# The last row tile of a decoder block behind its attention: halves on two engines, bf16 rows first

## The chip, the cores and the metric

The kernel runs on one core of a Trainium2 chip. A core has TensorE (PE, matrix products into PSUM), VectorE (DVE), ScalarE (ACT), GpSimd (POOL) and SyncE (SP, which here only starts transfers), each with its own stream of instructions; they wait for each other through semaphores. Sixteen DMA engines move data between the chip's memory and the on-chip SBUF. The metric is the device time of one execution in microseconds (us).

## The reference

Sixteen sequences of 112 rows (1792 rows in all, 1024 columns) go through three sub-layers. Each adds its result to its input and normalizes the row.

```python
x = _layernorm(x + _L0_attn_ref(x, w_gate, w_up, w_down))          # gated FF, half of each row set to 0
x = _layernorm(x + _L0_xattn_ref(x, ctx, ctx, Wq, Wk, Wv, Wo))     # 32 heads over 375 context rows
x = _layernorm(x + _L0_ffn_ref(x, qweight, qscale, qzeros))        # one 4-bit 1024x1024 matrix, in bf16

def _layernorm(x, axis=-1, eps=1e-05):
    m = jnp.mean(x, axis=axis, keepdims=True)
    v = jnp.var(x, axis=axis, keepdims=True)
    return (x - m) / jnp.sqrt(v + eps)
```

The last two of these lines end a row's work. The second one's output is rounded to bf16 for the third's matrix product, and is also added to that product in fp32.

## The kernel before, in words

The rows are cut into 14 tiles of 128 (`TT`), numbered 0 to 13. The program has one section after the other: gate, keys and values, up (`gates_keys_up`), down projection and first normalization (`Down`), and then `attention_and_ffn` (L772), which ends the kernel. A context manager, `as_written`, ties the instructions of each engine into the order in which the code writes them; so what stands ahead of an instruction on its engine is what the code wrote ahead of it.

`attention_and_ffn` goes over 128 units (sequence, half of the heads, one of four queries per key head). `scores` (L819), `normalize`, `square` and `values` (L876) are a unit's steps. When the sequences that fill a row tile are through, a `Tail` (L906) does the rest of that tile:

- `project` (L918) multiplies by `wo_sb`, a quarter of the columns at a time, and adds the result to the tile's fp32 row `xt`. For the last tile, number 13, `project_halves` (L933) does it in two parts, by the halves of the heads, into one PSUM tile `pp_last`; its two adds are at L944.
- `stats` (L946) calls `norm_stats` (L65): two `bn_stats` of 512 columns (L72), `bn_aggr` (L73) and the addition of `EPS` (L74) on VectorE, the power -0.5 on GpSimd (L75). GpSimd then makes `shift` = -mean * rstd (L949).
- `apply` (L953): ScalarE makes x * rstd + shift over all 1024 columns, in place in `xt` (L954).
- `normed` (L958): `apply`, then a VectorE cast of the row to bf16, `xb` (L961).
- `turn` (L963): TensorE transposes the eight 128-column parts of `xb` (columns j, j+8, ...) into one PSUM bank (L968); ScalarE copies the bank to `x2T` (L969).
- `packed` (L971): for each of two 512-column halves, eight bf16 matmuls `x2T` by `wf_sb` (L975), a ScalarE copy of the result to bf16 in `xb` (L980), and a GpSimd add to `xt` (L982).
- `stats` again, and `store` (L984): `apply`, and a 512 KB DMA of the tile to `out` from ScalarE's queue (L986).

For all tiles but the last, `piece` (L1011) and `lights` (L1031) hang these steps between the units: `behind` holds the matmul steps, `light` the others by the number of the unit behind which they are due.

Behind the last unit (L1081 and on) the order is written out by hand. The tiles 11 and 12 are finished there, and tile 13 begins. After `project_halves(1, pp)` come, in this order: tile 13's `stats` and `normed`; a loop that empties `behind` and `light`, which at this point holds tile 12's second `stats` and its `store`; tile 13's `turn`, `packed`, `stats` and `store`. PSUM banks come from a pool of three (`bank`, L800); `xb` and `x2T` have one buffer each.

Of the kernel before, what the change touches and what calls it, by code (L numbers as in the profile page):

```python
# [10 lines left out]
F32 = mybir.dt.float32  # L11
BF16 = mybir.dt.bfloat16
# [4 lines left out]
AF = mybir.ActivationFunctionType  # L17
ALU = mybir.AluOpType
# [4 lines left out]
P = 128  # L23
B, S, D = 16, 112, 1024
# [16 lines left out]
EPS = 1e-5  # L41
# [18 lines left out]
def layer_norm(nc, pool, y, out, negh):  # L60

    norm_apply(nc, y, out, *norm_stats(nc, pool, y, negh))


def norm_stats(nc, pool, y, negh):  # L65

    n = y.shape[0]
    st = pool.tile([P, 2, 6], F32, tag="ln_st", name="ln_st")
    mv = pool.tile([P, 2], F32, tag="ln_mv", name="ln_mv")
    rstd = pool.tile([P, 1], F32, tag="ln_rstd", name="ln_rstd")  # L70
    for i in range(2):
        nc.vector.bn_stats(st[:n, i, :], y[:, ts(i, D // 2)])  # L72
    nc.vector.bn_aggr(mv[:n], st[:n].rearrange("p a b -> p (a b)"))  # L73
    nc.vector.tensor_scalar(rstd[:n], mv[:n, 1:2], EPS, None, ALU.add)  # L74
    nc.gpsimd.tensor_tensor(rstd[:n], rstd[:n], negh[:n], ALU.pow)  # L75
    return mv[:n, 0:1], rstd[:n]


def norm_apply(nc, y, out, mean, rstd):
# [692 lines left out]
def attention_and_ffn(nc, tc, ident, ident_b, negh, x1_d, k_d, v_d, queries, wf_sb, wo, out):  # L772
# [16 lines left out]
    with ExitStack() as ctx:  # L789
# [4 lines left out]
        work = ctx.enter_context(tc.tile_pool(name="a_work", bufs=2))  # L794
        small = ctx.enter_context(tc.tile_pool(name="a_small", bufs=3))
# [4 lines left out]
        def bank():  # L800
            return ps.tile([P, 512], F32, tag="pg", name="bank")
# [104 lines left out]
        class Tail:  # L906
# [39 lines left out]
            def stats(self):  # L946
                mean, self.rstd = norm_stats(nc, small, self.xt, negh)
                self.shift = small.tile([P, 1], F32, tag="shift", name=f"shift_{self.t}")
                nc.gpsimd.tensor_scalar(  # L949
                    self.shift, mean, self.rstd, -1.0, ALU.mult, ALU.mult  # L950
                )
# [19 lines left out]
            def packed(self):  # L971
                for i in range(2):
# [8 lines left out]
                    x = self.xt[:, ts(i, 512)]  # L981
                    nc.gpsimd.tensor_tensor(x, x, yb, ALU.add)  # L982

            def store(self):  # L984
                self.apply()
                nc.scalar.dma_start(out[ts(self.t, P), :], self.xt)  # L986
                Tail.live -= 1
# [65 lines left out]
        for n in range(n_units):  # L1053
            b, c, r = units[n]
# [29 lines left out]
        n = n_units  # L1084
# [3 lines left out]
        tail = Tail(TT - 1)  # L1088
# [14 lines left out]
        values(n - 1)  # L1103
        step(n + 4)
        tail.project_halves(1, pp)
        tail.stats()
        tail.normed()
        n += 1
        n += 4
        while behind or light:  # L1110
            piece(n)
            lights(n)
            n += 1
        tail.turn()
        tail.packed()
        tail.stats()
        tail.store()


@with_exitstack  # L1120
def kernel(
# [34 lines left out]
    with as_written(nc, tc):  # L1156
        with ExitStack() as psum:
# [30 lines left out]
            for mc in range(EARLY):  # L1188
                queries.chunk(0, mc)
        attention_and_ffn(nc, tc, ident, ident_b, negh, x1_d, k_d, v_d, queries, wf_sb, wo, out)  # L1190


# [46 lines left out]
```

## Time and profile before

| | us |
|---|---|
| median of three runs | 2659.86 |
| the three runs | 2656.11, 2660.22, 2659.86 |
| the profiled execution, its own time | 2661.48 |
| its span, first to last instruction | 2659.7 |
| TensorE busy in the span | 2584.9 (97%) |
| VectorE, ScalarE, GpSimd busy | 1730.8, 1377.6, 1053.8 |
| end of tile 13's last projection matmul (L938), from the span's start | 2634.10 |
| start of tile 13's first matmul by `wf_sb` (L975) | 2644.82 |
| issue of the last store (L986) | 2655.95 |
| mean granted TensorE clock | 0.983 |

The page of a profile gives busy times, the chain of work that ended last (followed back from the end), and groups of instructions. A line of the view in order of time has the start in us from the start of the span, the duration in us, the engine (PEld is TensorE's weight load, a q behind the name its queue), the line of the code, the operation, what it writes and reads, the shapes, and in brackets how long the engine had been idle and which instruction ended that. A line of the groups has the engine, the operation, shapes and count, then the sum of busy time in us and the mean of one in ns, then the idle time before them. In the view by stretches of time the columns are named where it is shown.

### The profile page before, as it was taken

How to read it: one execution, taken by the hardware profiler on the slowest of the kernel's cores; microseconds unless marked ns; L12 is line 12 of the kernel's file. 1: busy time of each engine (PE TensorE's matmuls, PEld its weight loads, DVE VectorE, ACT ScalarE, POOL GpSimd, SP SyncE). 2: the span in 40 equal slices, each digit the busy share in tenths (PEclk: the TensorE clock that was granted, in tenths of full speed). 3: DMA queues.
4: the chain of work that ended last, by engine and by line, in shares of the span. 5: the costliest groups of instructions: out<-in, count | busy, mean ns of one | idle time of the engine just before them, and what ended most of it. 6: DMA issues, size and time to landing. Idle time of an engine off the chain costs nothing.

```text
span 2659.7 us, 33179 instructions
## 1 busy us (share of the span) xinstructions
PE 2584.9 (97%) x10266; PEld 1482.7 (56%) x10266; DVE 1730.8 (65%) x3579; ACT 1377.6 (52%) x2413; POOL 1053.8 (40%) x1097
## 2 busy tenths in 40 slices
PE   9999999999999999999999999998899999999997
PEld 4444444577776555555554444443556666667663
DVE  0478778866876788788730343158467777777773
ACT  0487787777767777787610000000255555565553
POOL 0002022213322444344450000023277888788783
PEclk9999999999999999999999999999889999999998
DMA  6221223154443543443346222166567777777763
GB/s 253 94 74 56 77 91 126 51 195 168 181 169 136 162 140 121 143 132 117 95 145 228 86 96 94 59 204 202 133 169 196 196 191 193 192 205 194 188 175 103
DMA packets 216960, 387.70 MB, mean 146 GB/s; under 512 B 32080, under 2 KB 151120, under 8 KB 212688
## 3 DMA queue, kind: packets, MB, share of 16 engines
q1 hardware_dynamic: 165456, 257.19, 32.3%
q0 software_dynamic: 35840, 100.59, 11.6%
q10 hardware_dynamic: 15488, 27.80, 3.5%
q8 instruction: 83, 1.36, 0.2%
q14 instruction: 93, 0.76, 0.1%
HBM read 208.36 MB, written 76.43 MB: 107 GB/s over the span
## 4 chain that ended last, share of the span: by engine, by line
PE 90%; DVE 3%; DMA 3%; ACT 2%; issue 1%; POOL 1%; ACTq 0%; SPq 0%; POOLq 0%; DVEq 0%
PE pg L146 20%; PE pu L234 19%; PE m L546 14%; PE bank L924 7%; PE pk L184 6%; PE pk L176 6%; PE bank L765 6%; PE sc L832 4%; PE po L887 3%; PE bank L975 2%; PE pt L255 1%; ACT probs L840 1%; DVE b L727 1%; DMA xr<-x_d 1%; DVE nmax L838 1%
## 5 line engine op out<-in xcount | busy, mean ns | idle before, releaser
L284 ACT ACTIVATE ja<-a,cand 128x1824 int8<-128x1824 f32 x434 | 788.6, 1817 | 178.4 <-DVE cand L296 174.4
L287 DVE TENSOR_SCALAR_CACHE_REDUCE jv<-a,cand 128x928 uint8<-128x928 f32 x434 | 510.0, 1175 | 56.9 <-ACT a L271 48.8
L234 PE MATMUL pu<-wu_sb,uxT 128*128 128x512 f32 (+1 forms) x1344 | 530.6, 548 | 0.0
L146 PE MATMUL pg<-wg_sb,gxT 128*128 128x456 f32 (+1 forms) x1344 | 519.9, 550 | 5.9 <-DMA wg_sb<-in_wg_dram 5.9
L840 ACT ACTIVATE probs<-sc,nmax 128x375 f32<-128x375 f32 x512 | 287.4, 573 | 237.6 <-DVE nmax L838 218.2
L146 PEld LDWEIGHTS pg<-wg_sb,gxT 128*128 128x128 f32 x1344 | 256.2, 191 | 268.8 <-issue 265.3
L849 POOL TENSOR_TENSOR probs<-probs,sums 128x1500 f32<-128x1500 f32 x128 | 344.2, 2689 | 142.4 <-DVE sums L848 123.2
L234 PEld LDWEIGHTS pu<-wu_sb,uxT 128*128 128x128 f32 x1344 | 249.0, 190 | 230.0 <-issue 188.4
L838 DVE TENSOR_REDUCE nmax<-sc 128x2 f32<-128x750 f32 x256 | 228.6, 932 | 150.3 <-PE sc L832 150.2
L546 PE MATMUL m<-wd,h 128*128 128x512 f32 (+1 forms) x616 | 268.0, 597 | 0.0
L860 DVE STREAM_TRANSPOSE squares<-probs 128x1536 f32<-128x1536 f32 x128 | 224.0, 1750 | 9.7 <-DMA weights<-squares 5.5
L155 POOL DMA_DIRECT2D s_d<-s x84 | 46.0, 548 | 427.4 <-DVE s L154 351.5
L765 PE MATMUL bank<-x1T,wq_sb 128*128 128x224 f32 x976 | 202.6, 361 | 0.0
L546 PEld LDWEIGHTS m<-wd,h 128*128 128x128 f32 (+1 forms) x616 | 117.5, 191 | 149.2 <-issue 145.1
L765 PEld LDWEIGHTS bank<-x1T,wq_sb 128*128 128x128 f32 x976 | 181.3, 191 | 33.2 <-issue 30.2
L924 PE MATMUL bank<-wo_sb,aT 128*128 128x256 f32 x832 | 195.0, 388 | 0.0
L758 ACT COPY x1T<-pq 128x448 f32<-128x448 f32 x4 | 2.0, 535 | 371.6 <-PE pq L757 371.6
L874 POOL DMA_DIRECT2D weights<-squares x320 | 178.6, 564 | 9.0 <-issue 6.6
L924 PEld LDWEIGHTS bank<-wo_sb,aT 128*128 128x128 f32 x832 | 155.4, 192 | 46.5 <-issue 24.9
L184 PE MATMUL pk<-wv_sb,ctx 128*128 128x256 f32 (+1 forms) x768 | 168.4, 379 | 0.0
L176 PE MATMUL pk<-ctx,wk_sb 128*128 128x375 f32 x512 | 164.4, 478 | 0.0
L184 PEld LDWEIGHTS pk<-wv_sb,ctx 128*128 128x128 f32 (+1 forms) x768 | 144.0, 188 | 24.8
(118 smaller groups left out, 2881.8 us busy)
## 6 DMA issues: line engine op xcount, KB each, us to landing
weights<-squares SPq DMA_DIRECT2D x704, 96.0 KB, 3.3
h<-hT_d SPq DMA_DIRECT2D x56, 640.0 KB, 4.5
weights<-squares POOLq DMA_DIRECT2D x320, 96.0 KB, 3.4
ctx<-in_ctxT_dram SPq DMA_DIRECT2D x16, 1500.0 KB, 6.7
a<-s_d SPq DMA_DIRECT2D x14, 1376.0 KB, 7.9
us<-s_d SPq DMA_DIRECT2D x56, 256.0 KB, 2.7
hT_d<-hT POOLq DMA_DIRECT2D x56, 256.0 KB, 3.1
s_d<-s POOLq DMA_DIRECT2D x56, 228.0 KB, 2.2
```

The costliest lines, as they stand in the source:

```text
L146: nc.tensor.matmul(pg[:, :w], xts[t][:, kc, :], wg_sb[:, kc, ds(off, w)], start=(kc == 0), stop=(kc == KC - 1),)
L176: nc.tensor.matmul(pk[:, :SK], wk_sb[:, kc, ts(u, P)], c[:, kc, :], start=(kc == 0), stop=(kc == KC - 1),)
L184: nc.tensor.matmul(pk[:n, :KVD], c[:, kc, ds(at, n)], wv_sb[:, kc, :], start=(kc == 0), stop=(kc == KC - 1),)
L234: nc.tensor.matmul(pu[:, :w], xts[t][:, kc, :], wu_sb[0][:, kc, ds(off, w)], start=(kc == 0), stop=(kc == KC - 1),)
L284: nc.scalar.activation(ja, a[:, NV:], AF.Sign, bias=cand, scale=-1.0, accum_out=st["sgn"])
L287: nc.vector.tensor_scalar(jv, a[:, :NV], cand, -(TOPK - 1 - NA / 2), ALU.is_lt, ALU.add, accum_out=st["nlt"])
L546: self.nc.tensor.matmul(bank, a[:r, k, :], b(k)[:r], start=(k == 0), stop=(k == HK - 1),)
L765: nc.tensor.matmul(pq[:, :GT], self.wq_sb[:, kc, ts(mc, P)], self.x1T[g][:, kc, :], start=(kc == 0), stop=(kc == KC - 1),)
L838: nc.vector.tensor_reduce(nmax[h], sc[h][:, :, :SK], AX.X, ALU.max, negate=True)
L840: nc.scalar.activation(pr[:, i, :SK], sc[i // 2][:, i % 2, :SK], AF.Exp, bias=nmax[i // 2][:, i % 2 : i % 2 + 1], accum_out=sums[:, i : i ...
L849: nc.gpsimd.tensor_tensor(pr, pr, sums.unsqueeze(2).to_broadcast([P, 4, SK]), ALU.mult)
L924: nc.tensor.matmul(pp[:, :256], aT[:, h, r, :], wo_sb[:, h * REP + r, ts(i, 256)], start=(h == 0 and r == 0), stop=(h == 1 and r == REP - 1),)
```

## The change

`norm_stats` is cut in two: the part behind the `bn_stats` is now `norm_of`. After `project_halves(1, pp)` the loop over `behind` and `light` comes first, without the two steps of the count ahead of it, and then one new method, `last`, does all that is left of tile 13:

- `stats`, unchanged.
- The bf16 row `xb` comes straight from the fp32 row: ScalarE makes the first 512 columns, VectorE the other 512, both as x * rstd + shift. `xt` keeps its unnormalized values for now.
- The eight transposes go to two PSUM banks, four to each. ScalarE copies the first to `x2T[:, :4]`, VectorE the second to `x2T[:, 4:]`.
- The fp32 row is normalized in place behind that, again by halves on ScalarE and VectorE.
- For each 512-column half: eight matmuls, ScalarE's copy to bf16, an add on VectorE (not GpSimd), and that half's `bn_stats` right behind it.
- The last normalization by halves on ScalarE and VectorE, and two stores of 256 KB: the first half from ScalarE's queue, the second from SP's.

Other tiles are done as before. In the line numbers of the changed kernel, `last` is L988 to L1040.

```diff
+            def last(self):
+                n = D // 2
+                self.stats()
+                self.xb = work.tile([P, D], BF16, tag="xb", name="xb_last", bufs=1)
+                nc.scalar.activation(
+                    self.xb[:, :n], self.xt[:, :n], AF.Identity, bias=self.shift, scale=self.rstd
+                )
+                nc.vector.tensor_scalar(
+                    self.xb[:, n:], self.xt[:, n:], self.rstd, self.shift, ALU.mult, ALU.add
+                )
+                self.x2T = work.tile([P, 8, P], BF16, tag="x2T", name="x2T_last", bufs=1)
+                by_place = self.xb.rearrange("t (p j) -> t j p", j=8)
+                for h in range(2):
+                    pt = bank().bitcast(BF16)[:, : 4 * P].rearrange("p (j t) -> p j t", j=4)
+                    for j in range(4):
+                        nc.tensor.transpose(pt[:, j, :], by_place[:, 4 * h + j, :], ident_b)
+                    if h:
+                        nc.vector.tensor_copy(self.x2T[:, 4:], pt)
+                    else:
+                        nc.scalar.copy(self.x2T[:, :4], pt)
+                nc.scalar.activation(
+                    self.xt[:, :n], self.xt[:, :n], AF.Identity, bias=self.shift, scale=self.rstd
+                )
+                nc.vector.tensor_scalar(
+                    self.xt[:, n:], self.xt[:, n:], self.rstd, self.shift, ALU.mult, ALU.add
+                )
+                st = small.tile([P, 2, 6], F32, tag="ln_st", name="ln_st_last")
+                for i in range(2):
+                    pf = bank()
+                    for j in range(8):
+                        nc.tensor.matmul(
+                            pf, self.x2T[:, j, :], wf_sb[:, j, ts(i, n)],
+                            start=(j == 0), stop=(j == 7),
+                        )
+                    yb, x = self.xb[:, ts(i, n)], self.xt[:, ts(i, n)]
+                    nc.scalar.copy(yb, pf)
+                    nc.vector.tensor_add(x, x, yb)
+                    nc.vector.bn_stats(st[:, i, :], x)
+                mean, self.rstd = norm_of(nc, small, st, negh)
...
+                nc.scalar.activation(
+                    self.xt[:, :n], self.xt[:, :n], AF.Identity, bias=self.shift, scale=self.rstd
+                )
+                nc.scalar.dma_start(out[ts(self.t, P), :n], self.xt[:, :n])
+                nc.vector.tensor_scalar(
+                    self.xt[:, n:], self.xt[:, n:], self.rstd, self.shift, ALU.mult, ALU.add
+                )
+                nc.sync.dma_start(out[ts(self.t, P), n:], self.xt[:, n:])
...
         tail.project_halves(1, pp)
-        tail.stats()
-        tail.normed()
-        n += 1
-        n += 4
         while behind or light:
             piece(n)
             lights(n)
             n += 1
-        tail.turn()
-        tail.packed()
-        tail.stats()
-        tail.store()
+        tail.last()
```

More of the change, by code (lines that the diff above doesn't have):

```diff
@@ L65, in norm_stats, with norm_of @@
 def norm_stats(nc, pool, y, negh):
-    n = y.shape[0]
     st = pool.tile([P, 2, 6], F32, tag="ln_st", name="ln_st")
+    for i in range(2):
+        nc.vector.bn_stats(st[:, i, :], y[:, ts(i, D // 2)])
+    return norm_of(nc, pool, st, negh)
+def norm_of(nc, pool, st, negh):
     mv = pool.tile([P, 2], F32, tag="ln_mv", name="ln_mv")
     rstd = pool.tile([P, 1], F32, tag="ln_rstd", name="ln_rstd")
[L71 to L76, printed above, removed]
+    nc.vector.bn_aggr(mv, st.rearrange("p a b -> p (a b)"))
+    nc.vector.tensor_scalar(rstd, mv[:, 1:2], EPS, None, ALU.add)
+    nc.gpsimd.tensor_tensor(rstd, rstd, negh, ALU.pow)
+    return mv[:, 0:1], rstd
 def norm_apply(nc, y, out, mean, rstd):
@@ L982, in packed @@
                     nc.gpsimd.tensor_tensor(x, x, yb, ALU.add)
+            def last(self):
[25 more added lines that the diff above has]
+                st = small.tile([P, 2, 6], F32, tag="ln_st", name="ln_st_last")
+                for i in range(2):
+                    pf = bank()
[9 more added lines that the diff above has]
+                mean, self.rstd = norm_of(nc, small, st, negh)
+                self.shift = small.tile([P, 1], F32, tag="shift", name="shift_last")
+                nc.gpsimd.tensor_scalar(
+                    self.shift, mean, self.rstd, -1.0, ALU.mult, ALU.mult
+                )
[5 more added lines that the diff above has]
+                    self.xt[:, n:], self.xt[:, n:], self.rstd, self.shift, ALU.mult, ALU.add
+                )
+                nc.sync.dma_start(out[ts(self.t, P), n:], self.xt[:, n:])
```

## The prediction

> **What bounds the kernel now.** I read the page first, then the chain that ended last from 2560 us on, then the instructions in order of time from 2628 us to the end, then the groups with shapes kept apart, then the granted clock by stretches. The page says that the kernel as a whole belongs to TensorE:
>
> ```profile
> PE 90%; DVE 3%; DMA 3%; ACT 2%; issue 1%; POOL 1%; ACTq 0%; SPq 0%; POOLq 0%; DVEq 0%
> ```
>
> The reader is to see that little but PE ends the chain. The change touches nothing until the last projection matmul ends at 2634.10 us. All that it can win or lose lies in the 25.6 us from there to the end of the span, 2659.70 us, where one row tile is left and the engines work one behind the other:
>
> ```profile
> 2634.13 0.69 DVE L944 TENSOR_TENSOR x<-x,pp_last 128x512 f32<-128x512 f32 x1 [3.79 <-PE pp_last L938]
> 2634.73 1.28 DVE L72 BATCH_NORM_STATS2 ln_st<-x 128x6 f32<-128x512 f32 x2
> ...
> 2637.47 1.24 ACT L954 ACTIVATE x<-x,shift,ln_rstd 128x1024 f32<-128x1024 f32 x1 [10.67 <-POOL shift L949]
> 2638.74 0.69 DVE L961 CAST xb<-x 128x1024 bf16<-128x1024 f32 x1 [2.30 <-ACT x L954]
> 2639.35 1.28 DVE L72 BATCH_NORM_STATS2 ln_st<-x 128x6 f32<-128x512 f32 x2
> ...
> 2642.09 1.24 ACT L954 ACTIVATE x<-x,shift,ln_rstd 128x1024 f32<-128x1024 f32 x1 [3.39 <-POOL shift L949]
> 2643.37 0.34 ACTq L986 DMA_DIRECT2D out_dram<-x  x1
> 2643.75 1.01 ACT L969 COPY x2T<-bank 128x1024 bf16<-128x1024 bf16 x1 [0.42 <-ACT x L954]
> 2644.82 0.13 PEld L975 LDWEIGHTS <-x2T 128*128 128x128 bf16 x2 [4.50 <-ACT x2T L969]
> 2644.82 5.82 PE L975 MATMUL bank<-wf_sb,x2T 128*128 128x512 bf16 x16 [4.26 <-ACT x2T L969]
> ...
> 2651.34 1.15 POOL L982 TENSOR_TENSOR x<-x,xb 128x512 f32<-128x512 f32 x1 [1.06 <-ACT xb L980]
> 2652.52 0.69 DVE L72 BATCH_NORM_STATS2 ln_st<-x 128x6 f32<-128x512 f32 x1 [1.51 <-POOL x L982]
> ...
> 2654.67 1.24 ACT L954 ACTIVATE x<-x,shift,ln_rstd 128x1024 f32<-128x1024 f32 x1 [3.41 <-POOL shift L949]
> 2655.95 0.34 ACTq L986 DMA_DIRECT2D out_dram<-x  x1
> ```
>
> Three things are to be seen. The eight transposes end at 2639.49 + 1.07 = 2640.56 us, but their copy starts at 2643.75 us: ScalarE takes its work in order, and ahead of that copy stands the store of tile 12 (2642.09), which waits for statistics that VectorE began at 2639.35. That is 3.2 us of the path. Second, whole rows are done by one engine where two could share them (1.24, 0.69, 1.01, 1.24). Third, 9.05 us lie between the last matmul's end (2644.82 + 5.83 = 2650.65) and the end.
>
> **The change, step by step.** Times below are span times of the changed kernel, with the stretches of before where the shape stays.
>
> Up to the shift. Tile 12's statistics now stand ahead of tile 13's on VectorE, behind the same adds at L944. Tile 12 so takes the slots 2634.73 (bn_stats) to 2637.47 (ScalarE apply) that tile 13 had, and tile 13's bn_stats starts when L74 is issued: 2636.29 + 0.08 (at 2591.36 the next instruction followed L74 by 0.08) = 2636.37, which is **1.64 later**. Its shift releases ScalarE at 2637.47 + 1.64 = 2639.11. ScalarE meanwhile applies tile 12 (1.24) and issues its store, 2638.75 to 2639.09: it is free as the shift arrives, at 2639.13. Nobody waits for tile 12's store.
>
> The bf16 halves. The forms that give the prices:
>
> ```profile
> L954 ACT ACTIVATE x<-x,shift,ln_rstd 128x1024 f32<-128x1024 f32 x28 | 35.0, 1250 | 20.2 <-POOL shift L949 20.2
> L980 ACT CAST xb<-bank 128x512 bf16<-128x512 f32 x28 | 16.4, 591 | 14.5 <-PE bank L975 14.3
> L969 ACT COPY x2T<-bank 128x1024 bf16<-128x1024 bf16 x14 | 14.3, 1019 | 15.7 <-PE bank L968 15.2 <-ACT x L954 0.4
> L80 DVE TENSOR_SCALAR y<-y,ln_mv,ln_rstd 128x1024 f32<-128x1024 f32 x14 | 11.4, 813 | 9.9 <-POOL ln_rstd L75 9.9
> ```
>
> ScalarE at 512 against 1024 columns: 1.019 - 0.591 = 0.43 less, so the half apply is 1.25 - 0.43 = **0.82** (bounds 0.62, the half, and 1.25). VectorE's half: the 1024-column cast takes 0.69 and a 128-column one (L719) 0.22, 0.52 ns a column, so 0.81 - 0.27 = 0.54 (bounds 0.41 and 0.81). It lies beside ScalarE's half, which ends last: 2639.13 + 0.82 = 2639.95. In the built program neither half waits for the other.
>
> Transposes from 2640.00, as before 0.05 behind their input. Four end after 3 x 0.107 + 0.32 = 0.64 (0.107 is the spacing of the eight in 1.07). ScalarE's copy of half a bank is 0.59 (L980): 2640.68 to 2641.27, and the first matmul starts at **2641.33** instead of 2644.82. VectorE's copy of the other half, bounded by 0.35 (half a cast) and 0.69 (L944, which reads PSUM too), is wanted by the fifth matmul, 1.7 us later: hidden. The fp32 halves (0.82 and 0.54) lie beside the matmuls; without that cover they would cost 0.82. Gain so far 2644.82 - 2641.33 = **3.49**.
>
> The matmuls depend on the granted clock:
>
> ```profile
> 1935.90:1939.31 3.41, 3.41 (x11) 2.98 (x10) 2.77 (x4) 2.34 (x8) 1.99 (x1) 0.50 0.58 129
> ...
> 2639.06:2642.46 3.40, 1.07 (x8) 0.82 (x8) 1.93 (x5) 0.36 (x1) 0.81 (x2) 0.50 0.00 0
> 2642.46:2645.87 3.41, 1.05 (x3) 0.43 (x4) 0.00 (x0) 1.89 (x2) 0.00 (x0) 0.50 0.38 156
> 2645.87:2649.28 3.41, 3.41 (x9) 1.21 (x8) 0.00 (x0) 0.59 (x1) 0.16 (x1) 0.50 0.00 0
> ```
>
> Columns: stretch, length, busy time of PE, its loads, VectorE, ScalarE, GpSimd, granted clock, DMA. The clock is 0.50 until a stretch of 3.41 is all busy, and 1.00 in the next (from 2649.29; at 1929.07 and 1932.49 stretches with 3.09 and 2.87 busy were not enough, the one at 1935.90 was). A matmul is 0.427 apart at 0.50 and 0.227 at full clock (16 in 3.63). On the same grid of stretches the changed kernel's first full one is 2642.46 to 2645.87: 4.54 / 0.427 = 10.6 matmuls slow, 5.4 x 0.227 = 1.2 after it, 5.8 in all, as before. End 2647.16; gain here 0. Bounds, if the grid falls otherwise: 4.6 (a stretch that starts with the transposes) and 6.9 (16 x 0.427).
>
> Behind the matmuls. The first half's copy, add and bn_stats (0.59 + 0.68 + 0.69) hide beside the second half's matmuls. For the second: copy 0.59, then the add on VectorE, 0.68 (512-column fp32 tensor_tensor, L241 and L562; bounds 0.68 and GpSimd's 1.15), bn_stats 1.35 behind the last matmul where it was 2652.52 - 2650.65 = 1.87: gain **0.52**. From bn_stats to the apply 2.15, unchanged. The half apply on ScalarE 0.82 for 1.24; VectorE's ends at 0.54 and so issues the SP half first: 1.35 + 2.15 + 0.54 + 0.05 = 4.09 behind the last matmul, ScalarE's half at 4.36, where the whole store went at 5.30. SP has been idle since 2616. The store's packets ran from 2656.75 to about 2658.2 at 399 GB/s and below, 0.85 behind the issue; the span ended 3.75 behind it. I let the two halves share this rate, so the end is 4.09 + 3.75 = 7.84 behind the last matmul against 9.05: gain 1.21 (with the 0.52). If each had the full rate, it would be 0.4 less. [...]
>
> **Sum:** 3.49 + 0 + 1.21 = **4.7 us**. The profiled execution took 2661.48 (span 2659.70 and 1.8 around it), so it would take 2656.8. It lies 1.6 above the median of the three runs, 2659.86, which are 4.1 apart; on the median the forecast is 2659.86 - 4.7 = **2655.2**. What a measurement here can tell from no change is 0.2%, 5.3 us: the bounds are 2654.5 and 2665.2, and the forecast lies 0.7 inside.
>
> **Rivals.**
> 1. *The clock comes earlier.* If the grid falls so that one stretch holds the transposes and the matmuls (only 0.26 idle between them, where before had 4.26), the matmuls take down to 4.6: gain 4.7 + 1.2 = 5.9, time 2654.0. For: a grid that does not start with the kernel. Against: a stretch 3.09 of 3.42 busy was not enough. [...] No stretch here decides it.
> 2. *Halves cost what wholes do.* Apply halves of 1.25 (twice 0.43) and a late clock (6.9 - 5.8 = 1.1): gain 4.7 - 2.0 = 2.7, time 2657.2. Against: 0.59 and 1.02 for the two widths.
> 3. *The end is a late store.* The last half lands late on SP's queue. Price: the rows' longest landing of a 512 KB store is 9.0 us (L672) against 2.6 for the last one here, 6.4: time 2655.2 + 6.4 = 2661.6, slower; it decides from a landing of 2.6 + 4.7 = 7.3 us. For: two queues on one set of engines. Against: the DMA column is 0 ahead of it.
>
> That the change does less than it says is no rival: the built order has tile 12's store ahead and the halves apart.
>
> **How the numbers follow.** Forecast as summed (gain 4.0 to 5.3) 0.50, rival 1 0.30, rival 2 0.15, rival 3 0.05. Faster by over 0.2%: rival 1 and, since medians of runs 4 us apart scatter by about 1, a third of the forecast: 0.47. Within: the rest of the forecast, rival 2, part of rival 3: 0.50. Slower: 0.03. Range: low 2655.2 - 1.2 (clock) - 0.4 (halves of 0.62) - 0.4 (store) - 1.2 (scatter) = 2652.0; high 2657.2 + 0.8 (scatter) = 2658.0. Rival 3 is left out.
>
> **What would show it.** Tile 12's ScalarE apply near 2637.5, then the half at L994 near 2639.1 of 0.82; first L1020 matmul 7.2 behind the last L938 one; L1026 of 0.68; SP's issue 0.3 ahead of ScalarE's. I am wrong if the halves of L994 take over 1 us, if the 16 matmuls are far from 5.8, or if work ahead of 2634 moves.

## The result and the profile after

| | before | after |
|---|---|---|
| median of 22 runs each, us | 2657.57 | 2654.11 |
| lowest to highest | 2654.92 to 2663.45 | 2648.84 to 2657.43 |
| the profiled execution, its own time | 2661.48 | 2652.74 |
| its span | 2659.67 | 2650.93 |
| start of tile 13's last projection add (L944, L948) | 2634.13 | 2629.37 |
| from there to the end of the span | 25.55 | 21.55 |

The changed kernel is 3.46 us faster by the medians; the ratio on record is 0.9986, with a 95% interval from 0.998 to 0.9993. The interval lies below 1, so the change is faster; but the gain is smaller than the 0.2% that the prediction set as the least that can be told from no change here. The two profiled executions differ by more, 8.74 us, but 4.76 of it lies ahead of the last projection add, in instructions that the change doesn't touch. In the 13 kernels profiled for this study that add starts anywhere from 2628.35 to 2635.27 us. So the start is set aside as scatter, and everything below is measured from that add: the tail went from 25.55 to 21.55, **4.0 us less**.

The page's shares of the chain that ended last say the same as before, PE 89% for 90%, and can't show a change of 4 us. The view in order of time of the changed kernel, from the add to the end, answers to the first lines shown of before (columns as there):

```profile
2629.37 0.69 DVE L948 TENSOR_TENSOR x<-x,pp_last 128x512 f32<-128x512 f32 x1 [3.79 <-PE pp_last L942]
...
2632.72 1.24 ACT L958 ACTIVATE x<-x,shift,ln_rstd 128x1024 f32<-128x1024 f32 x1 [10.67 <-POOL shift L953]
...
2633.99 0.34 ACTq L1044 DMA_DIRECT2D out_dram<-x  x1
...
2634.35 0.55 DVE L997 TENSOR_SCALAR xb_last<-x,ln_rstd,shift 128x512 bf16<-128x512 f32 x1 [1.03 <-POOL shift L953]
2634.44 0.81 ACT L994 ACTIVATE xb_last<-x,shift,ln_rstd 128x512 bf16<-128x512 f32 x1 [0.48 <-POOL shift L953]
...
2635.31 1.07 PE L1005 MATMUL bank<-ident_b,xb_last 128*128 128x128 bf16 x8 [5.97 <-ACT xb_last L994]
2635.99 0.59 ACT L1009 COPY x2T_last<-bank 128x512 bf16<-128x512 bf16 x1 [0.74 <-PE bank L1005]
...
2636.63 4.45 PE L1020 MATMUL bank<-wf_sb,x2T_last 128*128 128x512 bf16 x10 [0.25 <-ACT x2T_last L1009]
...
2642.57 0.59 ACT L1025 CAST xb_last<-bank 128x512 bf16<-128x512 f32 x1 [1.73 <-PE bank L1020]
2643.20 0.69 DVE L1026 TENSOR_TENSOR x<-x,xb_last 128x512 f32<-128x512 f32 x1 [0.89 <-ACT xb_last L1025]
...
2646.08 0.82 ACT L1033 ACTIVATE x<-x,shift_last,ln_rstd 128x512 f32<-128x512 f32 x1 [2.92 <-POOL shift_last L1030]
2646.08 0.55 DVE L1037 TENSOR_SCALAR x<-x,ln_rstd,shift_last 128x512 f32<-128x512 f32 x1 [1.03 <-POOL shift_last L1030]
2646.66 0.35 SPq L1040 DMA_DIRECT2D out_dram<-x  x1
2646.93 0.34 ACTq L1036 DMA_DIRECT2D out_dram<-x  x1
```

Three things are to be seen. The copy of the transposes (L1009) no longer waits for tile 12: it starts 0.68 behind the first transpose, where before it stood 3.2 behind the last. The matmuls start 7.26 behind the add, where before it was 10.69. And between SP's issue and the end of the span there are 4.27 us, where before 3.73 lay behind the issue of the whole store.

The tail falls into three stretches: from the add to the first matmul by `wf_sb`, from there to the copy of the second half's result, and from there to the end. This table holds them for all kernels. Its last two columns are about the closing, the instructions behind the kernel's own work; the trace has them, most of them DRAIN and EVENT_SEMAPHORE, under one line at the program's end, L1286 in the changed kernel. `SyncE` is the time from the end of GpSimd's last computing instruction, the second `shift` of tile 13, to the end of SyncE's last closing instruction, which stands behind the landing of the stores (2649.63 in the changed kernel, where the later store landed 2.4 behind its issue at 2646.93). `closing` is the time from there to GpSimd's next instruction.

| kernel | to the first matmul | matmuls | copy to end | whole tail | SyncE | closing |
|---|---|---|---|---|---|---|
| before | 10.69 | 5.85 | 9.00 | 25.55 | 4.27 | 0.03 |
| after | 7.26 | 5.94 | 8.35 | 21.55 | 3.59 | 0.56 |
| e1_order | 9.28 | 5.03 | 9.00 | 23.31 | 4.27 | 0.03 |
| e2_halves | 9.04 | 5.15 | 8.35 | 22.54 | 3.59 | 0.57 |
| e3_early12 | 5.54 | 6.08 | 8.36 | 19.98 | 3.58 | 0.57 |
| e4_warm | 7.08 | 3.66 | 8.35 | 19.09 | 3.59 | 0.56 |
| e5_act_store | 7.26 | 5.29 | 8.35 | 20.90 | 3.86 | 0.29 |
| e6_one_store | 7.25 | 6.20 | 8.35 | 21.80 | 3.85 | 0.31 |
| e7_sp_store | 7.25 | 5.98 | 8.35 | 21.57 | 3.84 | 0.31 |
| e8_pool_add | 7.25 | 5.91 | 8.85 | 22.01 | 3.59 | 0.56 |
| e9_all | 4.89 | 3.66 | 8.35 | 16.90 | 3.60 | 0.55 |
| e10_act_end | 7.25 | 5.86 | 8.49 | 21.59 | 4.26 | 0.03 |
| e11_two_stores | 10.69 | 6.14 | 9.07 | 25.90 | 4.35 | 0.03 |

Where the work is the same, the first and the last stretch repeat to within 0.02 (7.25 and 7.26 in six kernels, 8.35 and 8.36 in eight; that three of these eight store in another way is taken up below). So single profiles can be compared there. A few matmul records are missing from the traces, so a line can count 15 of 16. The matmuls scatter with the clock, from 5.03 to 6.20 where nothing holds it up, and are read apart.

### The profile page after: what moved, and what is told of

The parts are those of the page before. It is cut to its first block, busy times and chain, and to the rows that moved or that the text cites. A ratio compares the mean times of both kernels' runs of the same rounds, so it can differ in the third digit from the quotient of the medians.

```text
span 2650.9 us, 33174 instructions
## 1 busy us (share of the span) xinstructions
PE 2579.0 (97%) x10252; PEld 1480.9 (56%) x10266; DVE 1732.0 (65%) x3584; ACT 1376.4 (52%) x2414; POOL 1051.7 (40%) x1095
## 4 chain that ended last, share of the span: by engine, by line
PE 89%; DVE 3%; DMA 3%; ACT 2%; issue 1%; ACTq 1%; POOL 0%; SPq 0%; POOLq 0%; DVEq 0%
PE pu L238 19%; PE pg L150 19%; PE m L550 14%; PE bank L928 7%; PE pk L188 6%; PE pk L180 6%; PE bank L769 6%; PE sc L836 4%; PE po L891 3%; PE bank L979 2%; PE pt L259 1%; ACT probs L844 1%; DMA xr<-x_d 1%; DVE nmax L842 1%; DMA wq_sb<-in_wq_dram 1%
```

## The experiments

The theory was that the first stretch gains from two things, the order (nobody waits for tile 12) and the halves, that the clock gives nothing, and that the end gains less than forecast. The rivals were that one of the two does it all, and that the second queue or VectorE's late half costs the rest.

**The order alone, and the halves alone.** In e1_order the kernel before gets only the new order:

```diff
-        tail.stats()
-        tail.normed()
-        n += 1
-        n += 4
         while behind or light:
...
+        tail.stats()
+        tail.normed()
         tail.turn()
```

In e2_halves the changed kernel has the old order: `last` is cut behind the bf16 halves, and its first part stands ahead of the loop.

```diff
         tail.project_halves(1, pp)
+        tail.first()
         while behind or light:
...
         tail.last()
```

> The kernel before with the order alone changed: tile 12's second statistics and its store stand ahead of tile 13's statistics; tile 13 is still done by whole rows. I measure in the profile the stretch from the start of the last projection add (L944) to the first matmul by wf_sb (10.69 us before, 7.26 in the changed kernel) and from that add to the end of the span (25.5 and 21.6). Theory: order and halves are two gains that add. The order takes 3.2 of ScalarE's wait away and costs 1.64 of VectorE's time, so the first matmul comes at 10.69 - 1.5 = 9.2 and the end at about 24.0. Rival: the order is the whole of the gain ahead of the matmuls and the halves are hidden: 7.3 and about 22.3. Second rival: the order alone gains nothing, as tile 13 starts 1.64 later and whole rows eat the rest: 10.7 and 25.5.

> The changed kernel with the old order: tile 13's statistics and its bf16 halves first, then tile 12's statistics and store, then the transposes' copies and all the rest by halves. Theory (two gains that add): tile 13's halves are ready 1.64 earlier than in the changed kernel, but ScalarE's copy of the first transposes stands behind tile 12's apply and store again; add to first matmul 8.9 us (a gain of 1.8 on 10.69), end at 23.2. Rival (order is the whole gain): 10.7 and 24.8. Rival (halves are the whole gain): 7.3 and 21.6.

To the first matmul e1 took 9.28 and e2 9.04: gains of 1.41 and 1.65, together 3.06, where both at once gain 3.43. Their own times were 2655.75 and 2656.52, with 2658.95 for a run of before beside them. The view in order of time of e1, around the transposes:

```profile
2634.00 1.24 ACT L954 ACTIVATE x<-x,shift,ln_rstd 128x1024 f32<-128x1024 f32 x1 [10.67 <-POOL shift L949]
...
2635.74 1.24 ACT L954 ACTIVATE x<-x,shift,ln_rstd 128x1024 f32<-128x1024 f32 x1 [0.50 <-POOL shift L949]
2637.01 0.69 DVE L961 CAST xb<-x 128x1024 bf16<-128x1024 f32 x1 [2.41 <-ACT x L954]
...
2637.76 1.07 PE L968 MATMUL bank<-ident_b,xb 128*128 128x128 bf16 x8 [7.14 <-DVE xb L961]
2638.87 1.01 ACT L969 COPY x2T<-bank 128x1024 bf16<-128x1024 bf16 x1 [1.89 <-PE bank L968]
```

Tile 12's apply (2634.00) is out of the way, and the copy follows the transposes; but whole rows stand one behind the other, 1.24, 0.69 and 1.01. The same view of e2:

```profile
2635.52 0.81 ACT L994 ACTIVATE xb_last<-x,shift,ln_rstd 128x512 bf16<-128x512 f32 x1 [10.68 <-POOL shift L953]
...
2636.39 0.71 PE L1010 MATMUL bank<-ident_b,xb_last 128*128 128x128 bf16 x8 [4.25 <-ACT xb_last L994]
...
2638.91 1.24 ACT L958 ACTIVATE x<-x,shift,ln_rstd 128x1024 f32<-128x1024 f32 x1 [2.58 <-POOL shift L953]
...
2640.57 0.59 ACT L1014 COPY x2T_last<-bank 128x512 bf16<-128x512 bf16 x1 [0.42 <-ACT x L958]
```

Here the transposes end at 2637.10, and the copy waits until 2640.57 for tile 12's apply and store. Two gains are left. VectorE's half no longer waits for ScalarE's whole row, so that tile 12's shift comes 6.71 behind the add (2638.88 - 2632.17) where before it was 7.94, 1.23 earlier; and the copy takes 0.59 for 1.01. That is 1.65. So both parts gain, and neither rival (the order alone, the halves alone) holds.

**What is still on the path.** In e3_early12 the loop that ends tile 12 stands ahead of `project_halves(1, pp)`, so that its statistics lie beside the last projection matmuls:

```diff
-        tail.project_halves(1, pp)
         while behind or light:
             piece(n)
             lights(n)
             n += 1
+        tail.project_halves(1, pp)
         tail.last()
```

> The changed kernel with the loop for tile 12 moved ahead of the last projection, so that tile 12's statistics and store lie beside TensorE's projection matmuls instead of ahead of tile 13's statistics. Theory: the changed kernel's order pays 1.64 us of VectorE's time on the path; here it is hidden, but the first of the two adds may start up to 0.15 late: add to first matmul 7.26 - 1.64 = 5.6, end at about 20.0 (clock as in the changed kernel), 21.6 - 1.6. Rival: tile 12's last add on GpSimd lands too late, VectorE waits in order and the adds and with them the last matmuls come 1 us or more later; then the stretch from the add is as short, but the idle time ahead of the first add is over 11.7 instead of 10.69.

The first stretch fell from 7.26 to 5.54, so the changed kernel still paid **1.72** for tile 12's statistics ahead of its own (forecast was 1.64 of delay). The rival, that tile 12's work holds up the two adds, doesn't hold: the first add's wait still ends with a projection matmul, and the second add starts 4.48 behind the first, as in the changed kernel. The time was 2653.16.

**The clock.** In e4_warm 24 matmuls whose result nobody uses stand behind the projection; they are work added.

```diff
         tail.project_halves(1, pp)
+        warm = bank()
+        for _ in range(24):
+            nc.tensor.matmul(warm, ident_b, wf_sb[:, 0, :512], start=True, stop=True)
```

> The changed kernel with 24 further bf16 matmuls (128x512, into a spare bank, their result is not used) behind the last projection matmul, 5.2 us of TensorE's time in which it is idle otherwise. Theory: the granted clock goes to 0.50 since a stretch of 3.41 us is idle; with these it stays at 1.00, the 16 matmuls take 3.6 us instead of 5.9 and the first four transposes 0.2 less: the stretch from the last add to the end is 21.6 - 2.3 - 0.2 = 19.1. Rival: the clock falls all the same, or the 16 matmuls wait for their 0.15 weight loads: no change, 21.6. Second rival: the extra matmuls hold up the transposes: longer than 21.6.

The one line of e4's view in order of time that matters:

```profile
2638.99 3.63 PE L1020 MATMUL bank<-wf_sb,x2T_last 128*128 128x512 bf16 x16 [0.43 <-ACT x2T_last L1009]
```

All 16 matmuls run 0.227 apart, and the second stretch takes 3.66 for 5.94. The granted clock is 0.50 from 2634.45 to 2641.28 in the changed kernel; in e4 it stays at 1.00 until 2646.29. The clock costs the changed kernel **2.3 us**, more than half of what the whole change won. The time was 2652.82.

Why the natural clock is late is seen in the views by stretches, cut along each kernel's own grid. The columns are stretch, length, busy time of PE, its loads, VectorE, ScalarE and GpSimd, granted clock, DMA share and rate. First e1, then e6 (of which below):

```profile
2639.33:2642.74 3.41, 2.81 (x7) 1.04 (x8) 0.00 (x0) 0.55 (x1) 0.00 (x0) 0.50 0.00 0
2642.74:2646.15 3.41, 2.14 (x9) 0.78 (x8) 0.69 (x1) 1.17 (x2) 1.67 (x2) 1.00 0.00 0
```

```profile
2636.20:2639.62 3.42, 2.82 (x13) 1.48 (x14) 0.88 (x2) 1.59 (x3) 0.00 (x0) 0.50 0.33 137
2639.62:2643.03 3.41, 3.41 (x10) 1.21 (x9) 0.87 (x2) 0.58 (x1) 0.00 (x0) 0.50 0.00 0
```

In e1 a stretch with 2.81 of matmuls was enough for the full clock in the next; in e6 a stretch with 2.82 was not. One difference is that 1.07 of e6's are the eight transposes. Without them 1.75 is left, and in e11 a stretch with 1.63 of matmuls alone (2644.17 to 2647.58) wasn't enough either. Whether the transposes count for less, these rows don't settle. How many matmuls ran slowly came of where the grid lay: in e1 the full clock came 2.81 behind the first of them and the second stretch took 5.03, in e6 it came 5.16 behind it (1.75 + 3.41) and the stretch took 6.20.

**The end: queues and engines.** Three kernels change the last stores of the changed kernel. In e5_act_store both halves go from ScalarE's queue; in e6_one_store and e7_sp_store one store of 512 KB goes behind both halves of the apply, from ScalarE's queue and from SP's.

```diff
 # e5_act_store
-                nc.sync.dma_start(out[ts(self.t, P), n:], self.xt[:, n:])
+                nc.scalar.dma_start(out[ts(self.t, P), n:], self.xt[:, n:])
 # e6_one_store, and with nc.sync e7_sp_store: both stores of halves replaced by
+                nc.scalar.dma_start(out[ts(self.t, P), :], self.xt)
```

> The changed kernel with both halves of the last store issued by ScalarE. In the changed kernel the span ends 4.27 us behind SP's issue where 3.75 were forecast; the packets and the landing are as forecast, but 1.55 us lie between SP's last wait for a landing and the end instead of 1.08. Theory: the closing handshake of the engines takes 0.47 longer because SP has issued a transfer shortly before it. Then here it is 1.1 again, while the second half is issued 0.35 behind the first: the end comes 3.7 to 4.0 behind ScalarE's first issue. Rival: two transfers under way on whatever queue cost it: 1.55 again. Second rival: it scatters from run to run and belongs to neither.

> The changed kernel with one store of 512 KB from ScalarE, behind both halves of the last apply. Theory (SP's issue costs 0.47 in the closing handshake): issue 0.3 later than SP's in the changed kernel, end 3.75 behind the issue as in the kernel before: 0.2 shorter than the changed kernel, 21.4 from the last add to the end. Rival (the split store is worth what was forecast): 21.9, 0.3 longer.

> The changed kernel with one store of 512 KB from SP, behind both halves of the last apply. Theory (SP's issue costs 0.47 in the closing handshake): the end comes 3.75 + 0.47 = 4.2 behind the issue, with 1.55 between the last wait and the end. Rival (two transfers cost it): 3.75 and 1.1.

All three end at 8.35 behind the copy, as the changed kernel does, with times of 2651.87, 2654.20 and 2655.60 (before beside them: 2655.89). What the early issue from SP wins is lost again: the closing takes 0.29 to 0.31 in them where it takes 0.56 with the split. In e7 SP alone issues, and the closing is as short as in e6, where SP issues nothing; so it isn't SP's issue that costs.

The trace shows what does set the end there: GpSimd's own closing. Its first closing instruction is one that the trace calls DRAIN, and two lines of the view by source line (L1286 of the changed kernel, up to 2650.1) show it beside SyncE's. The columns are line, queue (POOLq is GpSimd's), operation, count, shortest, median and longest duration in ns, and first and last start in us.

```profile
L1286 SPq DRAIN  x2: 7/7/7, 2649.6 to 2649.6; - x2
L1286 POOLq DRAIN  x1: 4422/4422/4422, 2645.7 to 2645.7; - x1
```

By the records to the hundredth, GpSimd's DRAIN runs from 2645.72 to 2650.15; SyncE is through at 2649.63; GpSimd goes on at 2650.19. In all 13 kernels this DRAIN takes 4.42 and ends 4.10 behind the end of GpSimd's last `shift`. In the nine kernels with a closing of 0.29 or more it ends behind SyncE, and GpSimd goes on 0.04 behind its end. In the four with 0.03 it ends 0.16 to 0.25 ahead of SyncE, and GpSimd goes on 0.03 behind SyncE. From there to the end it is 0.74 in all 13. So the later of the two sets the end, and `closing` is mostly the time by which GpSimd's DRAIN outlasts SyncE. In e5, e6, e7 and the changed kernel SyncE is through 3.84 to 3.86 and 3.59 behind the shift. They differ by 0.27 there, and nothing of it reaches the end.

e8_pool_add puts the 512-column adds back on GpSimd.

```diff
-                    nc.vector.tensor_add(x, x, yb)
+                    nc.gpsimd.tensor_tensor(x, x, yb, ALU.add)
```

> The changed kernel with the two last adds back on GpSimd. Theory: GpSimd's add of 512 columns takes 1.15 against 0.69 on VectorE, and only the second half's is on the path: the end 0.46 later, 22.0 from the last projection add to the end. Rival: the first half's add and statistics are on the path too, since nothing hides them: 0.9 later. Second rival: hidden, no change.

The end took 8.85, so the add on VectorE is worth **0.50** (forecast 0.52). This gain reaches the end, since the add stands ahead of GpSimd's last `shift`. The first half's add costs nothing on either engine. The time was 2655.74.

Then the two changes at the end were taken apart. e10_act_end gives the changed kernel the old end, ScalarE's whole row and one store; e11_two_stores gives the kernel before a split store, from ScalarE's and SP's queues, behind ScalarE's whole row.

```diff
 # e10_act_end: the two half applies and their stores replaced by
+                self.apply()
+                nc.scalar.dma_start(out[ts(self.t, P), :], self.xt)
 # e11_two_stores, on the kernel before
-        tail.store()
+        tail.apply()
+        nc.scalar.dma_start(out[ts(tail.t, P), : D // 2], tail.xt[:, : D // 2])
+        nc.sync.dma_start(out[ts(tail.t, P), D // 2 :], tail.xt[:, D // 2 :])
```

> The changed kernel with the end of the kernel before: the last apply whole on ScalarE and one store of 512 KB from it. Between SP's second closing step and GpSimd's next one lie 0.03 us in the kernel before and with the order alone, 0.30 with one store or with two from ScalarE behind an apply on both engines, 0.56 with stores from ScalarE and SP. Theory: 0.28 of it comes with VectorE's work at the very end, the rest with the second queue. Then 0.03 here, and the end 3.73 behind the issue; from the second half's copy to the end 8.35 + 0.14 = 8.5. Rival: the 0.28 comes with something else in the changed kernel (its length, the adds on VectorE): 0.30.

> The kernel before with the last store alone cut in two, half from ScalarE's queue and half from SP's; the last apply is whole on ScalarE. Theory (the second queue costs 0.27 in the closing steps and VectorE's late work 0.28): 0.30 between SP's second closing step and GpSimd's next. Rival: SP's issue costs the whole 0.53: 0.56. Second rival: nothing without VectorE's late work: 0.03. The stretch from the last projection add to the end stays within 0.5 of 25.5, as both halves start together and share the engines.

The closing was 0.03 in both. First the two DRAINs of e10 (by source line, up to 2654), then e11's last lines in order of time:

```profile
L1280 SPq DRAIN  x2: 7/10/13, 2653.8 to 2653.9; - x2
L1280 POOLq DRAIN  x1: 4423/4423/4423, 2649.3 to 2649.3; - x1
```

```profile
2657.36 0.35 SPq L1119 DMA_DIRECT2D out_dram<-x  x1
2657.36 0.38 ACTq L1118 DMA_DIRECT2D out_dram<-x  x1
```

In e10 GpSimd's DRAIN is as long as ever and ends at 2653.70; SyncE is through at 2653.86 and is the later one now. In e11 two queues issue at the same moment, SyncE is through 4.35 behind the shift, and the closing takes 0.03: a second queue by itself costs nothing there, and that rival falls. Nor does VectorE's late work cost the 0.28 that the two expectations gave it. The halves and the two queues bring SyncE's part forward, to less than the 4.10 at which GpSimd's DRAIN ends, and a wait that was hidden before shows.

The price is plain. The halves at the end were forecast to win 0.69 over ScalarE's whole row. Up to SyncE's last closing instruction they do win 0.67 (4.26 against 3.59 behind the shift), but at the end only 0.14 (8.49 against 8.35). The split by itself, in e11, loses 0.07 (9.07 against 9.00). Why the DRAIN takes 4.42, and whether it would end earlier with less or earlier work on GpSimd, no run shows: GpSimd's last work is the same in all 13 kernels. The times were 2656.41 and 2662.95, one run each.

**All that helped.** e9_all takes the changed kernel, e3's order, 15 unused matmuls behind the projection (work added, as in e4), and each half's `bn_stats` right behind its projection add:

```diff
                     if h == 1:
                         x = self.xt[:, ts(i, 512)]
                         nc.vector.tensor_add(x, x, pp[:, i, :])
+                        nc.vector.bn_stats(self.st[:, i, :], x)
...
-        tail.project_halves(1, pp)
         while behind or light:
             piece(n)
             lights(n)
             n += 1
+        tail.project_halves(1, pp)
+        warm = bank()
+        for _ in range(15):
+            nc.tensor.matmul(warm, ident_b, wf_sb[:, 0, :512], start=True, stop=True)
         tail.last()
```

> The changed kernel with what the experiments pointed to: tile 12's statistics and store ahead of the last projection, 15 further matmuls behind it that keep the clock up (result not used), and each half of tile 13's first bn_stats right behind its projection add, so that one of them hides beside the other half's matmuls. Theory (the gains add): from the last add to the first matmul 5.54 - 0.6 - 0.2 = 4.8, the sixteen matmuls 3.7, behind them 8.35: 16.8 to the end, against 21.55 in the changed kernel and 25.55 before; a time of 0.9967 of the kernel before. Rival: early work of tile 12 and the bn_stats hold up the two adds and so the last projection matmuls, which gives a microsecond or more back ahead of the add: the stretch is as short, the time 0.9975 or more. Second rival: the clock falls with 15 matmuls, 19.0 and 0.9975.

The tail is 16.90: 1.72 less by the order, 2.3 by the clock, and the rest by the first half's statistics, hidden now, and by faster transposes (0.71 for 1.07). In order of time:

```profile
2628.35 0.69 DVE L950 TENSOR_TENSOR x<-x,pp_last 128x512 f32<-128x512 f32 x1 [3.06 <-PE pp_last L944]
2629.07 0.69 DVE L951 BATCH_NORM_STATS2 ln_st<-x 128x6 f32<-128x512 f32 x1
...
2633.23 3.63 PE L1027 MATMUL bank<-wf_sb,x2T_last 128*128 128x512 bf16 x15 [0.43 <-ACT x2T_last L1016]
```

One `bn_stats` and not two follows the add, and the matmuls start 4.9 behind it at the full clock. The median of 11 runs was 2650.72, with 2656.58 for 15 runs of before beside them: the ratio on record is **0.9976**, interval 0.9967 to 0.9985. Its tail is the shortest here. The tail's 8.65 would be 0.9967, the edge of that interval; the medians give 5.86. No give-back is seen ahead of the add in the profile, and the times alone don't settle whether there is one.

## Why the prediction was right, and which term was off

- **Up to the shift, the halves, the transposes.** As forecast. Tile 12 took tile 13's slots (apply 3.35 behind the add, before 3.34), the ScalarE half took 0.81 for 0.82, VectorE's 0.55 for 0.54, its copy of half a bank 0.42 within 0.35 to 0.69. The first matmul came 7.26 behind the add for 7.20: a gain of 3.43 for 3.49. e1 and e2 show that both parts carry it.
- **The matmuls.** Forecast 5.8 and no gain, measured 5.94 and a loss of 0.09. That the two agree is in part luck: where the grid falls differs from kernel to kernel, and 5.03 to 6.20 came of it. The reason given, that a stretch must be all busy, was too strict: 2.81 of 3.41 was enough in e1. Rival 1 needed one stretch with the transposes and the matmuls in it to be enough; e6's, 2.82 busy with 1.07 of transposes, was not. Its direction was seen, though: with the grid well placed 5.03 to 5.29 came about (e1, e2, e5), not 4.6.
- **Behind the matmuls: the mis-sized term.** The forecast was a gain of 1.21 and it was 0.65. The issues came where they were put, 4.11 and 4.38 behind the last matmul for 4.09 and 4.36, and the add on VectorE gave its 0.50 (e8). The step that was mis-sized is the 3.75 from the first issue to the end, taken over from before as if the store alone set it: it was 4.27. Of the 0.5 more, 0.08 is a later landing; 0.46 lies behind the landing. There GpSimd's closing DRAIN, which the forecast does not have, ends 0.51 behind SyncE's last closing instruction. In the kernel before it had ended 0.17 ahead of it, so it cost nothing, and what changed behind the `shift` could win no more than 0.15. In the forecast's own terms: the last apply starts 1.35 + 2.15 = 3.50 behind the last matmul, the shift ends 0.03 ahead of that, and from there GpSimd's part needs 4.10 + 0.04 + 0.74 = 4.88. That gives 8.35 where 7.84 was forecast; 8.37 was measured.
- **The stores.** The two halves shared the rate, as forecast. In the view of the DMA queues, SP's queue alone takes 99.4% of the 16 engines from 2647.5 to 2648.1, and ScalarE's alone moves packets from 2648.4 on. The first half's packets fill the engines up to 2648.34, the second's run from 2648.18 to 2649.02, and both together take 1.52 for the single store's 1.43. So the split saved no transfer time here. Rival 3, a late landing of the last half, didn't come.
- **Rival 2**, halves that cost what wholes do, falls with 0.81 and 0.55.
- **The sum.** 3.43 - 0.09 + 0.65 = 4.0 in the tail for 4.7; the medians' 3.46, with an interval of 1.9 to 5.3 (0.07% to 0.2% of 2657.6), hold both. The forecast time of 2655.2 came within 1.1 of the measured 2654.11, partly by luck: it started from 2659.86, 2.3 above the median of 22 runs, and took off 4.7, 1.2 more than the medians differ by. That the gain stayed within 0.2% was about even by the forecast's own chances (0.50 against 0.47 for more).

## What to carry to other kernels

Look for the copy that stands behind another tile's work on the same engine (here it began 3.2 behind the last transpose): splitting the rows and taking that work away gave 1.65 and 1.41 apart and 3.43 together, and hiding it beside the matmuls gave 1.72 more. At the end of a kernel, price not only the issue and the transfer of the last store but what every engine still has to do in the closing. Here GpSimd's DRAIN ended 0.17 ahead of SyncE's last step in the kernel before, so halves on a second engine and queue could bring only 0.14 of 0.69; a gain ahead of GpSimd's last `shift`, as the add's 0.50, came through whole. And where TensorE has idled ahead of a last run of matmuls, ask first what the clock costs there; here it was 2.3 us, and matmuls on data already at hand kept it at 1.00 (e4, e9).

## What the runs showed of the hardware that was not expected

- GpSimd's first closing DRAIN takes 4.42 us in all 13 kernels, and no kernel ends less than 4.88 behind GpSimd's last `shift`: it is 4.88 in the nine where the DRAIN outlasts SyncE (after, e2 to e9), 5.03 to 5.11 in the four where SyncE is later (before, e1, e10, e11). Why it takes that long stays open.
- Not every busy TensorE stretch raises the clock: 2.81 of matmuls of 128 rows did (e1), 2.82 with 1.07 of transposes didn't (e6), and the 3.09 and 2.87 that the prediction names, which in the trace of before are matmuls of 32 rows (L832) and fp32 transposes (L757), didn't either. How the chip counts them is not settled beyond these rows.
